# An LSTM feeding a sign-weight network on one core: the last quarter of the last block's outputs in two groups of four steps

## The chip, the cores and the metric

The kernel runs on one core of a Trainium2 chip. The metric is device time in microseconds. Of one execution there is also a profile, taken by the hardware profiler: every instruction of each engine with its start and length, the DMA packets, and the clock that TensorE was granted. A second run of the same kernel differs by a few tenths of a microsecond.

## What is computed

Inputs are 32 sequences of 64 steps of 256 numbers. An LSTM with 256 cells runs over the steps, and its hidden states go through three dense layers whose weights are signs; the result is added to the input.

```python
def lstm(x, h, Wx, Wh, b):              # x: (32, 64, 256)
    c = 0
    for t in range(64):
        i, f, o, g = split(x[:, t] @ Wx + b + h @ Wh, 4)
        c = sigmoid(f) * c + sigmoid(i) * tanh(g)
        h = sigmoid(o) * tanh(c)
        hs[:, t] = h
    return hs

def ffn(h, k0, k1, k2, s0, s1, s2):     # k: booleans, True = +1, False = -1
    a = relu(s0 * concat([h, -h]) @ sign(k0)) * 2     # 512 -> 1024
    a = relu(s1 * a @ sign(k1)) * 2                   # 1024 -> 1024
    return s2 * a @ sign(k2)                          # 1024 -> 256

out = x + ffn(lstm(x, cond, Wx, Wh, b), ...)
```

## The kernel before, in words

**Blocks.** The 64 steps are cut into four blocks of 16 steps (`SB`), that is 512 columns (`TB`; one column is one step of one sequence). The LSTM runs step by step; the network of block b runs on TensorE in the gaps of the LSTM of later blocks. The order of every engine's instructions is the order in which the program is written (`tc.manual_schedule()`), so a wait holds up whatever stands behind it on its engine.

**Precision.** The LSTM's products are in full float32. The network's are in a reduced float32 (`F32R`, 4 bytes, one pass of TensorE): each activation is split into a high and a low part (names ending in h and l), and each weight tile of 128 x 128 is multiplied by both. Every matmul in the profile is a pair of a weight load (LDWEIGHTS, engine column PEld) and a MATMUL (engine column PE). An instruction in full float32 appears as two such pairs.

**The last block.** The network of the last 16 steps (`last_block`) has no LSTM beside it any more; it is the end of the program. It works on two halves of eight steps (256 columns, `CB`). Its second layer is done by Strassen's method in quadrants (`product`, `take`, `take_sum`) and leaves the activations `a1[k, half]`, for eight tiles k and the two halves, as high and low tiles.

**The last layer of the last block**, where the change lies: the 256 outputs are two tiles m of 128, in the order that a 32 x 32 turn wants. `layer2(half, m, ...)` (L561) adds up, for one half and one m, eight tiles k times two parts: 16 matmuls of 256 columns. For the first half both m go into the two halves of one PSUM bank. For the second half m = 0 goes to a bank of `po`, and m = 1 to a bank of the pool `ps_f`. After that come, on VectorE, `turn_out` (L385, a transpose in 32 x 32 blocks from PSUM to SBUF) and `scale_out` (L388, times the product of the scales, plus the input x). The first half is turned twice, scaled once as 512 columns and stored while TensorE works on. In the second half each m is turned and scaled as soon as its 16 matmuls are done; when both are through, `store` (L380) sends the half out: four DMAs of 64 KB, one for each quarter of the 256 outputs, alternately from the queues of SyncE (SP) and ScalarE (ACT). Each is a set of pieces of 256 bytes.

```python
        for m in range(2):
            layer2(1, m, [*range(K2, FC0), *range(K2)], True, True)
            turn_out(os[1], po_half[1, m], m)
            scale_out(os[1][:, :, m, :], xq[b, 1][:, :, ts(m, 32)])
        store(b, 1, os[1].rearrange("p t m j -> p t (m j)"), [nc.sync, nc.scalar])
```

**After the last store** SyncE goes through all completion counters of the DMAs, one waiting instruction after another in a fixed order of counters, and then the engines meet twice (L764). Nothing of this is in the kernel's text. DMAs of the two hardware queues take their completion counters from eight in turn.

Of the kernel before, what the change touches and what calls it, by code (L numbers as in the profile page):

```python
# [32 lines left out]
F32 = mybir.dt.float32  # L33
# [8 lines left out]
def lstm_ffn(ctx: ExitStack, tc: tile.TileContext, x, cond, wx_d, wh_d, b_d, k0_d, k1_d, k2_d, s0_d, s1_d, s2_d, out):  # L42
    nc = tc.nc
    P = 128
    N, T, D = x.shape
# [3 lines left out]
    HQ = H // NQ  # L49
    F0 = k0_d.shape[1]  # L50
    F1 = k1_d.shape[1]
    FC0, FC1 = F0 // P, F1 // P
    SB = 16
    NB = T // SB
    TB = SB * N
# [22 lines left out]
    ps_f = ctx.enter_context(tc.tile_pool(name="ps_f", bufs=4, space=PSUM))  # L78
# [3 lines left out]
    def act(shape, dtype, name):  # L82
        return apool.tile(shape, dtype, tag="act", name=name)


    xq = {}
# [25 lines left out]
    first = warm[:, 4 : 4 + N]  # L112
# [47 lines left out]
    for i in range(2):  # L160
        t = act([P, 2, F0], U8, f"k0_{i}")
# [203 lines left out]
    def output(b, po):  # L365

        for half in range(2):
            o = act([P, SB // 2, 2, 32], F32, f"o{b}_{half}")
            for m in range(2):
                turn_out(o, po[m][:, ts(half, TB // 2)], m)  # L370
                yield
            o = o.rearrange("p t m j -> p t (m j)")
            scale_out(o, xq[b, half])
            store(b, half, o, [nc.sync])
            yield

    def store(b, half, o, engines):
        t0 = b * SB + half * (SB // 2)
        for q in range(NQ):
            engines[q % len(engines)].dma_start(  # L380
                out=out[:, t0 : t0 + SB // 2, ts(q, HQ)], in_=o[q * N : (q + 1) * N]
            )

    def turn_out(o, p, m):
        nc.vector.transpose(o[:, :, m, :], p.rearrange("p (t n) -> p t n", n=N))  # L385

    def scale_out(o, res):
        nc.vector.scalar_tensor_tensor(o, o, total, res, ALU.mult, ALU.add)  # L388


    K2, F2, CB = FC0 // 2, F1 // 2, TB // 2
# [25 lines left out]
    def last_block(b):  # L417

        hi, lo = hparts.pop(b)
        full, b11, b2, t, a1 = [], {}, {}, {}, {}  # L420
# [55 lines left out]
        for m in range(FC0):  # L476
            p = ps_f.tile([P, TB], F32, tag="pf", name=f"p0_{b}_{m}")
            for n, (k, a) in enumerate(((0, hi), (0, lo), (1, hi), (1, lo))):
                nc.tensor.matmul(p, w0[:, k, ts(m, P)], a[:, k, :], start=(n == 0), stop=(n == 3))  # L479
            f = act([P, 2, CB], F32, f"f_{m}")  # L480
            full.append(f)
            nc.scalar.activation(f.rearrange("p c n -> p (c n)"), p, AF.Relu)
            if m < K2:
# [3 lines left out]
                f = f[:, 0]  # L487
# [16 lines left out]
        q = [g.rearrange("p (i n) -> p i n", i=2) for g in gate_banks]  # L504
# [39 lines left out]
        for pair in range(2):  # L544
# [2 lines left out]

        po = [ps_o.tile([P, TB], F32, tag="po", name=f"po{b}_{m}") for m in range(2)]  # L550
        po_half = {
            (0, 0): po[0][:, :CB],
            (0, 1): po[0][:, CB:],
            (1, 0): po[1][:, :CB],
            (1, 1): ps_f.tile([P, TB], F32, tag="pf", name=f"po{b}_2")[:, :CB],
        }

        def layer2(half, m, ks, first, last):
            for k in ks:
                for n in range(2):  # L560
                    nc.tensor.matmul(  # L561
                        po_half[half, m],
                        w2[:, m, k],
                        a1[k, half][n],
                        start=first and k == ks[0] and n == 0 and (half, m) != (0, 1),
                        stop=last and k == ks[-1] and n == 1,
                        skip_group_check=True,
                    )

        os = [act([P, SB // 2, 2, 32], F32, f"o{b}_{half}") for half in range(2)]  # L570
        for ks in (range(K2), range(K2, FC0)):
            for m in range(2):
                layer2(0, m, ks, ks[0] == 0, ks[0] > 0)
        for m in range(2):
            turn_out(os[0], po_half[0, m], m)
        o = os[0].rearrange("p t m j -> p t (m j)")
        scale_out(o, xq[b, 0])
        store(b, 0, o, [nc.sync, nc.scalar])
        for m in range(2):
            layer2(1, m, [*range(K2, FC0), *range(K2)], True, True)  # L580
            turn_out(os[1], po_half[1, m], m)
            scale_out(os[1][:, :, m, :], xq[b, 1][:, :, ts(m, 32)])
        store(b, 1, os[1].rearrange("p t m j -> p t (m j)"), [nc.sync, nc.scalar])

    def ffn_block(b):
        hi, lo = hparts.pop(b)
# [98 lines left out]
    def ffn():  # L685
        for b in range(NB - 1):
            yield from ffn_block(b)
        yield from last_block(NB - 1)
# [13 lines left out]
    for t in range(T):  # L702
# [22 lines left out]
        else:  # L725
            if t >= FIRST_CHORE and chores:
                part = chores.popleft()()
# [40 lines left out]
```

## Time and profile before

| | |
|---|---|
| time, median of 3 runs | 312.36 us (312.21 to 312.55) |
| time of the profiled execution | 312.31 us |
| its span (first to last instruction) | 310.5 us |
| granted TensorE clock, mean | 0.998 |
| PE busy | 304.5 us, 98% of the span |
| PEld busy | 242.7 us, 78% |
| VectorE (DVE) busy | 178.1 us, 57% |
| ScalarE (ACT) busy | 142.0 us, 46% |
| matmuls of the last layer of the last block (L561) | 64, from 298.26 to 305.95 us |
| the program's last stores issued | 306.97 us and after |

The time of the profiled execution is longer than its span by 1.8 us, which lie before the first and after the last instruction. Matmuls overlap: the length of one is its passage through the array, and the rate is read from the distance between two starts. The ends of matmuls are modelled by the profiler. Starts are counted from the beginning of the span.

### The profile page before, as it was taken

Reading aid. Unit: us, or ns where it says so; the run is one execution under the profiler, and the core shown is the slowest. Engines: PE = TensorE matmul, PEld = TensorE weight load, DVE = VectorE, ACT = ScalarE, POOL = GpSimd, SP = SyncE. Lnnn points to the kernel's source line nnn. Section 1 sums busy time; section 2 is a strip of 40 time slices with the busy share of each in tenths; the row PEclk is TensorE's granted clock in tenths of the full one; section 3 lists DMA queues with packets and bytes.
Section 4 is the critical chain, followed back from the end, with each engine's and each line's share of the span. In section 5 each row is a group of like instructions: output and inputs, shape, how many; then the busy total and the mean of one; then the engine's idle time right before and its main releaser. Section 6 shows DMA issues by size and latency. Waiting matters only on the chain.

```text
span 310.5 us, 9798 instructions
## 1 busy us (share of the span) xinstructions
PE 304.5 (98%) x4138; PEld 242.7 (78%) x4138; DVE 178.1 (57%) x530; ACT 142.0 (46%) x512; POOL 6.6 (2%) x24
## 2 busy tenths in 40 slices
PE   8999999999999999999999999999999999999994
PEld 4888888788777777777777777777777777899993
DVE  2566767777673444355754445567554434698543
ACT  0225566774564543435633434355443333886220
POOL 5300000000000000000000000000000000000000
PEclk9999999999999999999999999999999999999999
DMA  6874001142000000000010000000310000131002
GB/s 192 206 196 99 5 19 38 36 95 65 3 2 0 2 2 0 3 2 0 2 38 22 14 3 0 2 2 13 92 34 2 3 0 2 31 79 27 2 0 69
DMA packets 30587, 10.89 MB, mean 35 GB/s; under 512 B 27720, under 2 KB 29768, under 8 KB 30544
## 3 DMA queue, kind: packets, MB, share of 16 engines
q1 hardware_dynamic: 27136, 8.66, 11.2%
q10 hardware_dynamic: 3168, 1.57, 2.0%
q8 instruction: 32, 0.52, 0.7%
q0 software_dynamic: 240, 0.04, 0.1%
q14 instruction: 11, 0.09, 0.1%
HBM read 8.16 MB, written 2.10 MB: 33 GB/s over the span
## 4 chain that ended last, share of the span: by engine, by line
PE 97%; DVE 1%; ACT 0%; issue 0%; ACTq 0%
PE p L617 30%; PE gates L305 20%; PE px L246 18%; PE p L591 8%; PE po L604 7%; PE gates L452 4%; PE po L561 2%; PE r L452 2%; PE x L452 2%; PE p L479 2%; PE p_idle L643 1%; PE gates L641 0%; DVE a_7l L362 0%; DVE o L388 0%; PE p_bias L658 0%
## 5 line engine op out<-in xcount | busy, mean ns | idle before, releaser
L305 PEld LDWEIGHTS gates<-wh,hist 128*32 128x32 f32 x2016 | 54.6, 109 | 22.3 <-issue 13.4
L305 PE MATMUL gates<-wh,hist 128*32 128x192 f32 x2016 | 68.1, 275 | 0.0
L246 PE MATMUL px<-wx,xT 128*32 128x256 f32 (+1 forms) x1168 | 60.5, 353 | 0.1
L322 ACT ACTIVATE sig<-gates 128x128 f32<-128x128 f32 x64 | 17.7, 277 | 80.6 <-PE gates L305 80.4
L246 PEld LDWEIGHTS px<-wx,xT 128*32 128x32 f32 x1168 | 42.4, 110 | 11.3 <-DVE c_first L652 0.7
L326 DVE TENSOR_TENSOR kept<-sig,c 128x64 f32<-128x64 f32 x63 | 14.2, 225 | 50.0 <-ACT sig L322 49.7
L332 ACT ACTIVATE th<-c 128x64 f32<-128x64 f32 x64 | 16.4, 257 | 31.4 <-DVE c L330 31.4
L334 DVE TENSOR_TENSOR h<-sig,th 128x64 f32<-128x64 f32 x64 | 14.4, 225 | 20.7 <-ACT th L332 20.7
L262 DVE TENSOR_TENSOR xg<-px,bias 128x512 f32<-128x512 f32 x32 | 21.2, 671 | 2.8 <-PE px L246 2.3
L316 ACT COPY gates<-xg 128x192 f32<-128x192 f32 x64 | 20.0, 313 | 1.3 <-DVE xg L262 1.3
L591 PE MATMUL p<-hhi,w 128*128 128x512 f32 x48 | 19.3, 402 | 0.0
L591 PE MATMUL p<-hlo,w 128*128 128x512 f32 x48 | 19.1, 398 | 0.0
L339 DVE STREAM_TRANSPOSE hist<-h 128x64 f32<-128x64 f32 x64 | 15.7, 245 | 2.4
L330 DVE TENSOR_TENSOR c<-kept,new 128x64 f32<-128x64 f32 x64 | 14.4, 224 | 2.2
L324 ACT ACTIVATE sig<-gates 128x64 f32<-128x64 f32 x64 | 14.9, 233 | 0.1
L323 ACT ACTIVATE cand<-gates 128x64 f32<-128x64 f32 x64 | 14.0, 218 | 0.0
L328 DVE TENSOR_TENSOR new<-sig,cand 128x64 f32<-128x64 f32 x64 | 13.9, 217 | 0.0
L317 ACT COPY gates<-xg 128x64 f32<-128x64 f32 x64 | 13.0, 203 | 0.0
L591 PEld LDWEIGHTS p<-hhi,w 128*128 128x128 f32 x48 | 9.0, 188 | 2.2
L591 PEld LDWEIGHTS p<-hlo,w 128*128 128x128 f32 x48 | 9.0, 188 | 2.0
L211 ACT ACTIVATE w<-bits,nsgn,sgn 128x1024 fp32r<-128x1024 uint8 x8 | 9.9, 1241 | 0.0
L617 PE MATMUL p<-a_7h,w 128*128 128x512 f32 x24 | 9.9, 413 | 0.0
(249 smaller groups left out, 602.8 us busy)
## 6 DMA issues: line engine op xcount, KB each, us to landing
x<-in_x_dram SPq DMA_DIRECT2D x60, 64.0 KB, 2.8
out_dram<-o SPq DMA_DIRECT2D x28, 64.0 KB, 1.8
bits<-in_L_ffn_k_dram SPq DMA_DIRECT2D x10, 128.0 KB, 3.2
wx<-in_L_cond_Wx_dram SPq DMA_DIRECT2D x2, 256.0 KB, 4.2
wx<-in_L_cond_Wx_dram ACTq DMA_DIRECT2D x4, 128.0 KB, 4.6
wh<-in_L_cond_Wh_dram ACTq DMA_DIRECT2D x2, 256.0 KB, 5.6
wh<-in_L_cond_Wh_dram SPq DMA_DIRECT2D x2, 256.0 KB, 6.2
k<-in_L_ffn_k_dram SPq DMA_DIRECT2D x2, 256.0 KB, 3.1
```

Source lines behind the costliest of these rows:

```text
L246: nc.tensor.matmul(p[q * N : (q + 1) * N, t % 2, slots], xT[i // 2, i % 2][:, s, k, :], wx_q[:, k, q, slots], start=start, stop=False, ski ...
L262: nc.vector.tensor_tensor(xg[t], p.rearrange("p t g j -> p t (g j)"), b, ALU.add)
L305: nc.tensor.matmul(g[q * N : (q + 1) * N], hT[:, k, :], wh_q[:, k, q, slots], start=False, stop=(k == 1), skip_group_check=True,)
L316: nc.scalar.copy(gates[0], x_t[:, :3])
L322: nc.scalar.activation(sig[:, 0:2, :], gates[0][:, 1:3], AF.Sigmoid)
L324: nc.scalar.activation(sig[:, 2, :], gates[1][:, 0], AF.Sigmoid)
L332: nc.scalar.activation(th, c, AF.Tanh)
L339: nc.vector.transpose(hT, h.rearrange("p (j b) -> p b j", b=2))
L452: nc.tensor.matmul(bank[pair][:, i], a(k)[:, ts(2 * pair + i, P)], b(k, n), start=first and i == 0 and k == 0 and n == 0, stop=last and k ...
L591: nc.tensor.matmul(p, w0[:, k, ts(m, P)], a[:, k, :], start=(n == 0), stop=(n == 3))
L604: nc.tensor.matmul(po[m], w2[:, m, k], a1[k][n], start=(k == 0 and n == 0), stop=(k == FC1 - 1 and n == 1))
L617: nc.tensor.matmul(p1[m], w1[:, k, ts(m, P)], a0[k][n], start=(k == 0 and n == 0), stop=(k == FC0 - 1 and n == 1),)
```

## The change

The m = 0 part of the second half stays as it was: 16 matmuls of 256 columns, one turn, one scaling. The m = 1 part ("the last half of the outputs of the last eight steps") is done in two groups of four steps, 128 columns each: 16 matmuls of 128 columns into a bank of its own, a turn of 128 columns, a scaling of 128 columns, and then a store of these four steps for all 256 outputs, four DMAs of 32 KB. Each group loads all its weights again. `store` takes the steps as a further argument, and `layer2` takes its target bank and its columns.

```diff
-    def store(b, half, o, engines):
+    def store(b, half, o, engines, part=slice(0, SB // 2)):
         t0 = b * SB + half * (SB // 2)
         for q in range(NQ):
             engines[q % len(engines)].dma_start(
-                out=out[:, t0 : t0 + SB // 2, ts(q, HQ)], in_=o[q * N : (q + 1) * N]
+                out=out[:, t0 + part.start : t0 + part.stop, ts(q, HQ)], in_=o[q * N : (q + 1) * N, part]
             )
...
         po = [ps_o.tile([P, TB], F32, tag="po", name=f"po{b}_{m}") for m in range(2)]
-        po_half = {
-            (0, 0): po[0][:, :CB],
-            (0, 1): po[0][:, CB:],
-            (1, 0): po[1][:, :CB],
-            (1, 1): ps_f.tile([P, TB], F32, tag="pf", name=f"po{b}_2")[:, :CB],
-        }
+        last_po = [ps_f.tile([P, TB], F32, tag="pf", name=f"po{b}_{2 + i}") for i in range(2)]

-        def layer2(half, m, ks, first, last):
+        def layer2(p, m, half, ks, first, last, cols=slice(0, CB)):
             for k in ks:
                 for n in range(2):
                     nc.tensor.matmul(
-                        po_half[half, m],
+                        p,
                         w2[:, m, k],
-                        a1[k, half][n],
-                        start=first and k == ks[0] and n == 0 and (half, m) != (0, 1),
+                        a1[k, half][n][:, cols],
+                        start=first and k == ks[0] and n == 0,
...
-        for m in range(2):
-            layer2(1, m, [*range(K2, FC0), *range(K2)], True, True)
-            turn_out(os[1], po_half[1, m], m)
-            scale_out(os[1][:, :, m, :], xq[b, 1][:, :, ts(m, 32)])
-        store(b, 1, os[1].rearrange("p t m j -> p t (m j)"), [nc.sync, nc.scalar])
+        o = os[1].rearrange("p t m j -> p t (m j)")
+        ks = [*range(K2, FC0), *range(K2)]
+        layer2(po[1][:, :CB], 0, 1, ks, True, True)
+        turn_out(os[1], po[1][:, :CB], 0)
+        scale_out(os[1][:, :, 0, :], xq[b, 1][:, :, :32])
+        for i in range(2):
+            steps, p = ts(i, SB // 4), last_po[i][:, : CB // 2]
+            layer2(p, 1, 1, ks, True, True, ts(i, CB // 2))
+            turn_out(os[1][:, steps], p, 1)
+            scale_out(os[1][:, steps, 1, :], xq[b, 1][:, steps, 32:])
+            store(b, 1, o, [nc.sync, nc.scalar], slice(i * SB // 4, (i + 1) * SB // 4))
```

The first half's calls of `layer2` and `turn_out` are written with the new arguments and do the same as before. After the change the lines of the last block move: `layer2`'s matmul is L557.

More of the change, by code (lines that the diff above doesn't have):

```diff
@@ L572, in last_block @@
             for m in range(2):
-                layer2(0, m, ks, ks[0] == 0, ks[0] > 0)
+                layer2(po[0][:, ts(m, CB)], m, 0, ks, ks[0] == 0 and m == 0, ks[0] > 0)
         for m in range(2):
-            turn_out(os[0], po_half[0, m], m)
+            turn_out(os[0], po[0][:, ts(m, CB)], m)
         o = os[0].rearrange("p t m j -> p t (m j)")
```

## The prediction

> **What bounds the kernel now.** I read the page first, its chain of work that ended last:
>
> ```profile
> PE 97%; DVE 1%; ACT 0%; issue 0%; ACTq 0%
> ```
>
> TensorE carries the chain to the end, and whatever it gains or loses in its last stage counts in full. So I asked for the chain from 298 us on:
>
> ```profile
> 298.26 7.69 PE po L561 x64
> 305.95 0.02 issue
> 305.98 0.46 DVE o L385
> 306.43 0.03 issue
> 306.46 0.48 DVE o L388
> ```
>
> The 64 matmuls of the last layer run without a gap for 7.69 us, 0.120 us each. Then the last turn and the last scaling follow one another, 0.46 and 0.48 us. The timeline of the end shows what hands over to what:
>
> ```profile
> 305.54 0.28 PE L561 MATMUL po<-c_1h,w 128*128 128x256 f32 x1
> ...
> 305.66 0.28 PE L561 MATMUL po<-c_1l,w 128*128 128x256 f32 x1
> 305.98 0.45 DVE L385 STREAM_TRANSPOSE o<-po 128x256 f32<-128x256 f32 x1 [0.95 <-PE po L561]
> 306.46 0.48 DVE L388 SCALAR_TENSOR_TENSOR o<-o,total,x 128x256 f32<-128x256 f32 x1
> 306.97 0.81 SPq L380 DMA_DIRECT2D out_dram<-o  x2
> 306.98 0.88 ACTq L380 DMA_DIRECT2D out_dram<-o  x2
> ```
>
> Starts of neighbouring matmuls are 0.12 us apart, the last begins at 305.66, and both queues issue two stores each, some 0.4 us per store. What follows is seen only in stretches of time (columns: length, busy engines, granted clock, DMA share, GB/s):
>
> ```profile
> 307.00:307.50 0.50, 0.00 (x0) 0.00 (x0) 0.00 (x0) 0.00 (x0) 0.00 (x0) 1.00 0.00 0
> 307.50:308.00 0.50, 0.00 (x0) 0.00 (x0) 0.00 (x0) 0.00 (x0) 0.00 (x0) 1.00 0.25 65
> 308.00:308.50 0.50, 0.00 (x0) 0.00 (x0) 0.00 (x0) 0.00 (x0) 0.00 (x0) 1.00 0.81 207
> 308.50:309.00 0.50, 0.00 (x0) 0.00 (x0) 0.00 (x0) 0.00 (x0) 0.00 (x0) 0.98 1.08 245
> 309.00:309.50 0.50, 0.00 (x0) 0.00 (x0) 0.00 (x0) 0.00 (x0) 0.00 (x0) 0.50 0.04 8
> ```
>
> Nothing moves until some 0.8 us after the issue; then the 256 KB take about 1.3 us at 200 to 250 GB/s, to 309.05 or so. Another 1.4 us go by until the span ends at 310.5. The end is thus a chain in series: matmuls, turn, scaling, issue, transfer, closing waits. The change makes the links after the matmuls shorter, and pays on TensorE.
>
> **TensorE: the term that decides.** Removed are 16 matmuls of 256 columns, added 32 of 128 columns with 16 weight loads more. The first of the 16 starts at 305.66 - 15 x 0.12 = 303.86. Before, the last one starts 15 x 0.12 = 1.80 us later; after, 31 x p, where p is the distance between starts at 128 columns. The trace has no reduced-float32 matmul of 128 columns, so p is bounded:
>
> - From below by streaming. The rows of 512 columns are 0.227 us apart (269.64, 269.87, 270.09 in L479), those of 256 columns 0.120. That is 0.107 per 256 columns and 0.013 fixed, which gives 0.067 at 128.
> - By the weight load. It is as long whatever the columns are. The groups by shape:
>
> ```profile
> L246 PEld LDWEIGHTS px<-wx,xT 128*32 128x32 f32 x1168 | 42.4, 110 | 11.3 <-DVE c_first L652 0.7 <-issue 0.4
> L591 PEld LDWEIGHTS p<-hlo,w 128*128 128x128 f32 x48 | 9.0, 188 | 2.0
> ```
>
> A load of 128 columns lasts 188 ns and one of 32 columns 110: 78 ns for 96 columns, 0.81 ns each, so 0.104 us of a full load are work that a second load can't share. Where TensorE starts after a wait, two loads stand directly behind one another:
>
> ```profile
> 81.03 0.19 PEld L591 LDWEIGHTS p<-hhi,w 128*128 128x128 f32 x1
> 81.03 0.50 PE L591 MATMUL p<-hhi,w 128*128 128x512 f32 x1
> 81.14 0.19 PEld L591 LDWEIGHTS p<-hlo,w 128*128 128x128 f32 x1
> ...
> 81.37 0.40 PE L591 MATMUL p<-hlo,w 128*128 128x512 f32 x1
> ```
>
> The second load starts 0.11 us after the first, though it waits for no data. At 256 columns the load (0.107) and the stream (0.107) are about equal, and the load hides; at 128 columns the stream is half as long and the load is not. I therefore expect p between 0.107 and 0.120 and take 0.112, near the row of two adjacent loads: 31 x 0.112 - 1.80 = **+1.67 us** (+1.52 to +1.92; by streaming alone +0.28). The last matmul's own passage is shorter by 128 of 256 columns: (0.389 - 0.283) / 2 = **-0.05**.
>
> The Trainium skill has a rule here that speaks against the change: "TensorE: Matmul & The Clock Gate", section "LDWEIGHTS (loading the stationary operand)", says that a load costs its columns over 1.2 GHz, whatever else is done, which is 0.107 us for 128; the loads 0.11 us apart agree. The same page, section "Back-to-back issue gap", gives about 0.081 us per matmul of 128 columns in a stream of loads and matmuls. By that figure the term would be an estimated +0.71 instead of +1.67, and my sum about +0.1 instead of +1.0; the two adjacent loads of this trace speak for the former.
>
> **VectorE.** The last turn is of 128 columns instead of 256. The rows: 245 ns at 64 columns (L339), 449 at 256, 1.06 ns per column, so -0.14. The last scaling: 752 ns at 512 columns, 484 at 256, 1.05 per column, so -0.13. Together **-0.27**. The first group's turn and scaling (about 0.32 + 0.35 us) cost nothing: TensorE meanwhile needs 16 x 0.112 = 1.8 us for the second group, in a bank of its own. m = 0 of this half is through at 305.03, before the first group's turn at about 305.8. Without that cover they would cost 0.67.
>
> **The transfer.** Four stores of 32 KB end the program instead of four of 64 KB. The first group's four are issued about 306.5, and at 0.4 us each two per queue are out by 307.4; the last four come about 308.3, so nothing queues behind them, and their packets (about 307.3 to 308.0) are over before the last ones' begin. Each queue's second store is issued 0.4 us after its first and starts moving 0.8 us later, thus not before 1.2 us; with 64 KB at 200 to 250 GB/s behind it, it ends some 1.5 us after the first issue instead of 2.1. The ends are 0 (if only fixed costs count) and -0.7 (if the time goes by bytes); I take **-0.55**, near the row by bytes, since the transfer is a solid block at full share.
>
> **The closing waits.** Eight completion counters are used in turn. With four stores more, the last store from ACT counts on another: read from the built instructions, on the one that SyncE waits for second and not sixth. All later waits are then behind the last landing. In the trace four such waits of L764 lie between 309.46 and 309.65, 0.06 us apart; four more are **+0.24** (0 to 0.3). The new waits of the last stores on the first half's stores are free: those were issued at 303.73 and moved by 306.0. The wait of the second group's bank is for a product of the second layer, long read.
>
> **Sum.** 1.67 - 0.05 - 0.27 - 0.55 + 0.24 = +1.04 us. On the profiled execution's 312.31 us this is 313.35; its median lies 0.05 higher, so I say 313.4 us, 0.33% slower, and the span 311.5. With the ends of the unknown costs this case reaches from +0.5 (1.52 - 0.05 - 0.27 - 0.7) to +1.8 (1.92 - 0.05 - 0.27 + 0.24), 312.8 to 314.2.
>
> **The rivals.**
>
> 1. *The load hides at 128 columns too.* Then p is 0.067 and the sum 0.28 - 0.05 - 0.27 - 0.55 + 0.24 = -0.35, or -0.74 with the best ends: 311.6 to 312.0, not slower. It decides from p = 0.078 downwards, where 31 p equals the 1.80 + 0.63 that the tail gives back. For it: the record of a load (192 ns) already overlaps the next at 0.120, so loads are pipelined in some part. Against it: two adjacent loads are never closer than 0.107 in this trace. Chance 0.12.
> 2. *Half-width matmuls lose the one-pass rate* and run like full float32. L246's 128 records of 128 columns take 4.03 us from 5.44 on, four at a time in separate column groups: 0.126 us per round, two records per product, 0.25 us. Then 31 x 0.25 - 1.80 = +5.95, the sum +5.3, 317.7 us (at 0.22, where the start of the kernel is not counted, +4.4). For it: no reduced-float32 matmul below 256 columns is in the trace, so nothing shows its rate. Against it: it is one instruction with the same type as its neighbours in the build, where full float32 is two. Chance 0.10.
> 3. *The tail doesn't shrink* because issue and landing, not bytes, set it: the main case without its 0.55, +1.6, 313.95 us. It lies in the main case's range, which has 0.78 in all.
>
> **How the numbers follow.** A measurement of this kernel tells apart about 0.2%, 0.62 us. The main case passes +0.62 in nearly nine parts of ten: 0.69 of its 0.78; with rival 2, slower is 0.79. The rest of the main case (0.09) and most of rival 1 (0.08) lie within 0.62 us: 0.17. The rest of rival 1, 0.04, is faster. The range goes from rival 1's middle, 312.0, to just above the main case's upper end, 314.3; outside are rival 2 (0.10), half of rival 1 (0.06) and a little for what I have not thought of.
>
> **What would show it.** In the timeline after: starts of the 128-column matmuls 0.107 to 0.120 us apart, with loads as far apart and PEld without gaps there; the last turn near 0.31 us and the last scaling near 0.35; two bursts of transfer, the second over about 1.5 us after its first issue; more of L764's waits behind the last landing. Starts 0.07 apart would make the prediction wrong to the fast side, two records per matmul or starts over 0.2 apart to the slow side; a second burst as long as before would move it to rival 3.

## The result

| | before | after |
|---|---|---|
| time, median of 6 runs each | 312.47 us (312.21 to 313.07) | 314.30 us (313.71 to 314.54) |
| ratio, 95% interval | | 1.0054 (1.0041 to 1.0067) |
| span of the profiled execution | 310.5 us | 312.5 us |

The change makes the kernel 0.5% slower. 313.4 us was predicted, with a range of 312.0 to 314.3.

### The profile page after: what moved, and what is told of

Read it like the earlier page. It is cut to its first block, busy times and chain, and to the rows that moved or that the text cites. A ratio compares the mean times of both kernels' runs of the same rounds, so it can differ in the third digit from the quotient of the medians.

```text
span 312.5 us, 9838 instructions
## 1 busy us (share of the span) xinstructions
PE 306.3 (98%) x4154; PEld 244.3 (78%) x4154; DVE 178.6 (57%) x532; ACT 142.1 (45%) x512; POOL 6.6 (2%) x24
## 4 chain that ended last, share of the span: by engine, by line
PE 95%; DMA 2%; DVE 1%; ACTq 0%; issue 0%; ACT 0%
PE p L619 30%; PE gates L305 20%; PE px L246 17%; PE p L593 8%; PE po L606 7%; PE gates L452 4%; PE po L557 3%; PE r L452 2%; PE x L452 2%; PE p L479 2%; DMA wx<-in_L_cond_Wx_dram 2%; ACTq L93 0%; DVE a_7l L362 0%; ACTq L127 0%; PE p_bias L660 0%
```

## The profile after

The page's chain still belongs to TensorE, now with a piece of DMA that was not in it before (it lies at the start of the program, as shown below):

```profile
PE 95%; DMA 2%; DVE 1%; ACTq 0%; issue 0%; ACT 0%
```

The end of the chain, from TensorE's last group on (start, length, what):

```profile
298.87 9.30 PE po L557 x80
308.17 0.02 issue
308.20 0.33 DVE o L385
308.52 0.03 issue
308.55 0.35 DVE o L388
```

80 matmuls in 9.30 us stand where 64 in 7.69 stood, which is +1.61. Turn and scaling have shrunk from 0.46 + 0.48 to 0.33 + 0.35. The timeline shows the rate, first where the shape changes and then at the end:

```profile
304.35 0.28 PE L557 MATMUL po<-c_1l,w 128*128 128x256 f32 x1
304.35 0.19 PEld L557 LDWEIGHTS po<-c_0h,w 128*128 128x128 f32 x1
304.47 0.22 PE L557 MATMUL po<-c_0h,w 128*128 128x128 f32 x1
304.47 0.19 PEld L557 LDWEIGHTS po<-c_0l,w 128*128 128x128 f32 x1
304.53 0.28 PE L557 MATMUL po<-c_0l,w 128*128 128x128 f32 x1
304.58 0.19 PEld L557 LDWEIGHTS po<-c_0h,w 128*128 128x128 f32 x1
304.64 0.27 PE L557 MATMUL po<-c_0h,w 128*128 128x128 f32 x1
...
306.41 0.32 DVE L385 STREAM_TRANSPOSE o<-po 128x128 f32<-128x128 f32 x1 [0.77 <-PE po L557]
306.76 0.35 DVE L388 SCALAR_TENSOR_TENSOR o<-o,total,x 128x128 f32<-128x128 f32 x1
...
307.77 0.28 PE L557 MATMUL po<-c_1h,w 128*128 128x128 f32 x1
307.82 0.19 PEld L557 LDWEIGHTS po<-c_1l,w 128*128 128x128 f32 x1
307.88 0.28 PE L557 MATMUL po<-c_1l,w 128*128 128x128 f32 x1
308.20 0.32 DVE L385 STREAM_TRANSPOSE o<-po 128x128 f32<-128x128 f32 x1 [1.08 <-PE po L557]
308.55 0.35 DVE L388 SCALAR_TENSOR_TENSOR o<-o,total,x 128x128 f32<-128x128 f32 x1
308.93 0.79 SPq L380 DMA_DIRECT2D out_dram<-o  x2
308.93 0.86 ACTq L380 DMA_DIRECT2D out_dram<-o  x2
```

At 256 columns a load starts together with the matmul before it, and both are 0.12 apart. From the second matmul of 128 columns on, the loads are 0.11 apart, each starts later than the matmul before it, and its own matmul follows 0.06 after the load's start instead of 0.12: the loads pace the engine. (The first gap between matmuls, 0.06, is this lead being used up once.) The first group's turn and scaling lie at 306.4 to 307.1 under the matmuls. What follows the last issue is again only to be seen by stretches (length, busy engines, granted clock, DMA share, GB/s):

```profile
309.50:310.00 0.50, 0.00 (x0) 0.00 (x0) 0.00 (x0) 0.00 (x0) 0.00 (x0) 0.59 0.35 86
310.00:310.50 0.50, 0.00 (x0) 0.00 (x0) 0.00 (x0) 0.00 (x0) 0.00 (x0) 0.50 0.58 138
310.50:311.00 0.50, 0.00 (x0) 0.00 (x0) 0.00 (x0) 0.00 (x0) 0.00 (x0) 0.50 0.18 39
```

128 KB move between 309.75 and 310.68, so for about 0.93 us; before, 256 KB took about 1.3. Half the bytes don't take half the time.

Now the links can be put side by side. A store lands when its completion counter is full; here that is the moment at which SyncE's wait for that counter ends. From the first matmul of the last quarter of the last layer (303.86 before, 304.47 after) to the end of the span:

| link, us | before | after |
|---|---|---|
| first to last matmul of the quarter | 1.80 | 3.41 |
| last matmul's start to last turn's start | 0.32 | 0.32 |
| last turn's start to last store's first issue | 1.00 | 0.73 |
| issue to last landing (to last packet) | 2.49 (2.12) | 2.26 (1.75) |
| last landing to the end | 1.07 | 1.32 |
| sum | 6.67 | 8.04 |

The stretch costs +1.37 us. The span grew by 2.0. The other 0.6 us is at the start, where the two kernels issue the same instructions. In the chain of waits of the kernel after:

```profile
2.19 5.80 DMA wx<-in_L_cond_Wx_dram
7.99 0.14 issue
8.13 1.95 PE px L246 x64
```

TensorE's second batch of 64 for the first product starts at 8.13, after a wait for a load of Wx; before, it starts at 7.51. From the bias matmul (9.26 before, 9.87 after) to the first matmul of the last quarter it is 294.6 us in both. The experiments show whether that shift belongs to the change.

## The experiments

Each kernel was profiled once and, but for one, timed in five rounds against the kernel before. The table has the same links for all (scaling in place of the turn where nothing is turned); "bias" is the start of the bias matmul, which stands for what the start of the kernel took.

| run | bias | first to last matmul | to last turn | turn to issue | issue to landing (last packet) | closing | sum | time against before, 95% |
|---|---|---|---|---|---|---|---|---|
| before | 9.26 | 1.80 | 0.32 | 1.00 | 2.49 (2.12) | 1.07 | 6.67 | |
| after | 9.87 | 3.41 | 0.32 | 0.73 | 2.26 (1.75) | 1.32 | 8.04 | 1.0054 (1.0041 to 1.0067) |
| after again | 10.18 | 3.41 | 0.32 | 0.73 | 2.22 (1.75) | 1.33 | 8.01 | 1.0044 (1.0032 to 1.0056) |
| matmuls alone | 9.16 | 3.41 | 0.31 | 1.00 | 2.50 (2.13) | 1.07 | 8.29 | 1.0063 (1.0051 to 1.0075) |
| rest alone | 9.54 | 1.80 | 0.94 | 1.00 | 2.28 (1.84) | 1.32 | 7.34 | 1.0018 (1.0009 to 1.0026) |
| light loads | 9.27 | 1.92 | 0.26 | 0.73 | 2.18 (1.77) | 1.32 | 6.42 | one run, 312.38 us |
| groups of 6 and 2 steps | 9.70 | 3.38 | 0.31 | 0.60 | 2.03 (1.59) | 1.32 | 7.65 | 1.0032 (1.0020 to 1.0044) |
| other counters | 9.91 | 3.41 | 0.32 | 0.73 | 2.20 (1.75) | 0.95 | 7.60 | 1.0045 (1.0033 to 1.0056) |
| a store for each m | 9.64 | 1.80 | 0.32 | 1.00 | 2.22 (1.80) | 1.32 | 6.66 | 1.0003 (0.9994 to 1.0011) |
| activations as weights | 9.04 | 1.78 | 0.31 | 0.51 | 2.84 (1.98) | 0.95 | 6.40 | 0.9990 (0.9981 to 0.9998) |
| the same, four instructions more | 9.79 | 1.78 | 0.32 | 0.51 | 2.10 (1.72) | 0.95 | 5.66 | 0.9966 (0.9953 to 0.9978) |
| the same, by sequence | 9.51 | 1.78 | 0.32 | 0.51 | 2.28 (1.92) | 0.95 | 5.85 | 0.9981 (0.9972 to 0.9990) |

**After again.** The kernel after, unchanged.

> The changed kernel once more, to see how much of its +2.0 us of span belongs to its end. In the first profile the end (from the first matmul of the last quarter to the end of the span) grew by 1.37 us (6.67 to 8.04), and the beginning (up to the first bias matmul) by 0.61 us (9.26 to 9.87), where TensorE waits for the weights Wx. Theory: the 0.61 us are chance of the loads at the start; the end is again 8.0 us, and the bias matmul starts anywhere between 9.2 and 10.0. Rival: the changed program starts later in every run; the bias matmul is at 9.8 to 9.9 again, and kernels with the same beginning as before (the third of this call) show 9.26.

The links come out the same within 0.04 us; the bias matmul comes at 10.18 instead of 9.87. In the twelve profiles it lies anywhere from 9.04 to 10.18 (wider than the 9.2 to 10.0 expected), among kernels that begin with the same instructions, early and late with the split matmuls (9.16, 10.18) and without (9.04, 9.79); from there to the last quarter it is 294.56 to 294.62 us in all but the last kernel of the table. So nothing ties the 0.6 us at the start to the change, and profiles are compared here by the sum of the links, not by their spans. What makes the start vary stays open; in the kernel after it is a load of Wx that TensorE waits for.

**Matmuls alone.** Two groups of matmuls, then turn, scaling and store as before.

```diff
-            layer2(p, 1, 1, ks, True, True, ts(i, CB // 2))
-            turn_out(os[1][:, steps], p, 1)
-            scale_out(os[1][:, steps, 1, :], xq[b, 1][:, steps, 32:])
-            store(b, 1, o, [nc.sync, nc.scalar], slice(i * SB // 4, (i + 1) * SB // 4))
+            layer2(p[:, ts(i, CB // 2)], 1, 1, ks, i == 0, True, ts(i, CB // 2))
+        turn_out(os[1], p, 1)
+        scale_out(os[1][:, :, 1, :], xq[b, 1][:, :, 32:])
+        store(b, 1, o, [nc.sync, nc.scalar])
```

> Only the matmuls are cut in two groups of 128 columns, into one bank; the turn, the scaling and the stores are whole as before. Theory: the spacing is 0.111 us, the last matmul starts 3.41 us after the first of the quarter instead of 1.80, and all that follows is as before: the end is 6.67 + 1.61 = 8.28 us, the whole +1.6 us against before, 0.25 more than the changed kernel's end. Rival (the second bank, or the wait on it, costs the spacing): below 0.1 us apart, end below 7.9 us.

The sum is 8.29, +1.62 on before, all of it in the first link. The whole time, 1.0063, is 1.97 us (1.60 to 2.35) of this call's 312.78 for before. So in the links this one part accounts for more than the whole loss, and the rest of the change gives back 0.25.

**Rest alone.** The last 16 matmuls whole, and after them the turns, scalings and stores by four steps.

```diff
+        layer2(p, 1, 1, ks, True, True)
         for i in range(2):
-            layer2(p, 1, 1, ks, True, True, ts(i, CB // 2))
-            turn_out(os[1][:, steps], p, 1)
+            turn_out(os[1][:, steps], p[:, ts(i, CB // 2)], 1)
```

> Only what follows the matmuls is cut in two groups of four steps; the 16 matmuls are whole as before. Theory: after the last matmul come turn, scaling, turn, scaling (2 x 0.70 instead of 1.00 us to the last issue), the transfer to its landing is shorter as in the changed kernel (2.26 instead of 2.49 us) and the closing waits are longer (1.32 instead of 1.07): the end is 6.67 + 0.40 - 0.23 + 0.25 = 7.1 us, +0.4 us. Rival (the tail's gain is real once the matmuls don't pay for it): 6.67 us or less.

Nothing covers the first group now. The chain of waits from 306 us on:

```profile
306.24 0.33 DVE o L385
306.57 0.03 issue
306.60 0.35 DVE o L388
306.95 0.24 DVE o L385
307.18 0.02 issue
307.21 0.35 DVE o L388
```

The second turn starts 0.62 later than the only turn before. And a cost came on top that I had left out: the scaling ends at 307.56, but SP's issue of the last store starts at 307.86, since SP is issuing the first group's stores until then; that is why "turn to issue" is 1.00 and not 0.70. The sum is +0.67. Smaller pieces at the end of a chain pay only if something covers the pieces before the last. TensorE's matmuls are that cover, and splitting them is what costs.

**Light loads.** After, but the weight tiles of the two groups have 64 columns instead of 128, except each group's first. It leaves 64 of the 128 outputs of this part unfinished.

```diff
+                    wide = P if not light or (k == ks[0] and n == 0) else P // 2
                     nc.tensor.matmul(
-                        p,
-                        w2[:, m, k],
+                        p[:wide],
+                        w2[:, m, k, :wide],
```

> The changed kernel, but of the 32 matmuls of 128 columns all except the first of each group load only 64 weight columns, so that 64 of the 128 outputs of the last quarter are left unfinished. Theory (the weight load sets the spacing): the load is half as long, starts come to 0.07 us apart (0.053 of streaming and 0.013 fixed), the 31 spacings take 2.1 to 2.3 us instead of 3.41. Rival (a matmul of 128 columns streams at half rate): starts stay 0.11 us apart, 3.4 us.

The timeline:

```profile
303.87 0.22 PE L558 MATMUL po<-c_0h,w 128*128 128x128 f32 x1
303.87 0.14 PEld L558 LDWEIGHTS po<-c_0l,w 128*64 128x64 f32 x1
303.93 0.22 PE L558 MATMUL po<-c_0l,w 128*64 128x128 f32 x1
303.93 0.14 PEld L558 LDWEIGHTS po<-c_0h,w 128*64 128x64 f32 x1
303.99 0.22 PE L558 MATMUL po<-c_0h,w 128*64 128x128 f32 x1
```

The same 128 columns stream, but with half the weight columns the matmuls are 0.060 us apart instead of 0.111, and load and matmul start together again. The one full load between the two groups stands out: the load behind it starts 0.109 later, the others 0.06. The edit halves a matmul's output rows together with its weight columns; for the load, and against the output, speak the two loads that the prediction shows at 81.03 and 81.14, 0.11 apart though the second waits for no result. So the weight load sets the 0.111, as the prediction said, and the sum is 6.42, 0.25 less than before: had the load been hidden, the change would have won by the links. The Trainium skill's page "TensorE: Matmul & The Clock Gate", section "LDWEIGHTS (loading the stationary operand)", has the rule that holds here (its 128 columns over 1.2 GHz are 0.107; measured 0.111). Its section "Back-to-back issue gap" gives 0.081 for 128 columns in a stream of loads and matmuls; for these 4-byte weights the trace has 0.111, and the measurement decides.

**Groups of 6 and 2 steps** instead of 4 and 4 (after with other bounds).

```diff
-        for i in range(2):
-            steps, p = ts(i, SB // 4), last_po[i][:, : CB // 2]
+        for i, (s0, s1) in enumerate(((0, 6), (6, 8))):
+            steps, p = slice(s0, s1), last_po[i][:, : (s1 - s0) * N]
```

> The changed kernel with groups of six and two steps (192 and 64 columns) instead of four and four. Theory (the load sets the spacing, whatever the columns below 256): 0.111 us in both groups, the last matmul 3.41 us after the first; turn and scaling of 64 columns are 0.07 us shorter each, the last stores of 16 KB land some 0.1 to 0.2 us earlier: end 7.7 to 7.8 us. Rival (the spacing goes with the columns, at half rate): 0.17 us at 192 and 0.07 at 64, the last matmul 3.7 to 3.8 us after the first.

The timeline in the second group, at 64 columns:

```profile
306.89 0.28 PE L557 MATMUL po<-c_0h,w 128*128 128x64 f32 x1
307.00 0.28 PE L557 MATMUL po<-c_0l,w 128*128 128x64 f32 x1
307.11 0.28 PE L557 MATMUL po<-c_0h,w 128*128 128x64 f32 x1
```

Behind each group's first gap, starts are 0.109 to 0.116 apart at 192 columns and 0.111 to 0.112 at 64. Rival 2 (a lower rate below 256 columns) is out: what a matmul streams, from 64 to 192 columns, doesn't matter here. Once the matmuls are paid for twice, the last group may as well be small: its shorter tail makes the sum 7.65 instead of 8.04, still 0.98 above before.

**Other counters.** After, with six of the eight loads of x for the last block cut in two, so that the last stores take the counters that SyncE waits for last.

```diff
-            load_x(b, half, [nc.sync])
+            ...
+            for q in range(NQ):
+                for part in (slice(0, 4), slice(4, 8)) if q < 3 else (slice(0, 8),):
+                    nc.sync.dma_start(out=xq[b, half][q * N : (q + 1) * N, part], in_=...)
```

> The changed kernel with six more loads of x some 30 us before the end (six of the last block's eight loads are cut in two), which only moves the last stores to other completion counters: ScalarE's last store counts on the one that SyncE waits for last but one, not second. Theory (a later counter in the closing round saves 0.061 us each): from the last landing to the end of the span 1.32 - 6 x 0.061 = 0.95 us, the end of the kernel 7.65 us instead of 8.03. Rival (the closing stretch is a fixed 1.3 us, or is set by the landing itself): unchanged, 8.0 us.

The closing falls from 1.32 to 0.95, six waits of 0.061 us that now lie ahead of the last landing. SP's waits from 308 us on, after first, then this kernel (who waited for what, us in total, times, longest):

```profile
SPq L766 <- DMA out_dram<-o: 1.4, 1, 1.4
```

```profile
SPq L773 <- DMA out_dram<-o: 0.9, 2, 0.5
```

One long wait, with seven counters behind it, has become two, the second of them with one counter behind it. In the sum of the links it is -0.41 on the run "after again". The whole time doesn't show it (1.0045 against 1.0044, each within 0.0012, that is 0.37 us): the mechanism is shown by the profile, its worth in the whole time is not.

**A store for each m.** On the kernel before: each m is stored as soon as it is scaled, in pieces of 128 bytes, so that the last stores carry half the bytes, without any change to the matmuls.

```diff
             scale_out(os[1][:, :, m, :], xq[b, 1][:, :, ts(m, 32)])
-        store(b, 1, os[1].rearrange("p t m j -> p t (m j)"), [nc.sync, nc.scalar])
+            store_m(b, 1, os[1], m, [nc.sync, nc.scalar])
```

> The kernel before, whole matmuls, but each m of the second half is stored by itself as soon as it is scaled: four DMAs of 32 KB in pieces of 128 bytes for m = 0, beside the matmuls of m = 1, and four at the end. The last stores have half the bytes and as many pieces. If the transfer goes by bytes, it lands 2.26 us after the first issue as in the changed kernel (2.49 before), and with 0.25 us more of closing waits the end is 6.67 - 0.23 + 0.25 = 6.7 us, no change. If it goes by pieces, 2.49 us and 6.9 us, 0.25 us slower than before.

The last packet comes 1.80 us after the issue: as after (1.75, as many bytes in pieces of 256), not as before (2.12, as many pieces but twice the bytes). So the number of pieces is not what counts. The gain of 0.27 in landing is paid out again: four more stores move the last one to another counter, closing +0.25. Sum and time are those of before.

**Activations as weights.** On the kernel before: the last half is computed the other way round. The 128 columns of four steps are the stationary operand and the 256 outputs move. A group of four steps then costs 16 matmuls of 256 columns, both groups 32, as many as before; the result has a row for each step and sequence and needs no turn.

```diff
+                        a1[k, 1][n][:, ts(i, CB // 2)],
+                        w2[:, :, k].rearrange("p m (q j) -> p q m j", q=NQ),
...
+            nc.vector.scalar_tensor_tensor(o[:, i], p, total, x_rows[:, i], ALU.mult, ALU.add)
+            for s in range(SB // 4):
+                (nc.sync, nc.scalar)[s % 2].dma_start(out=rows[:, s], in_=o[ts(s, N), i])
```

> The kernel before with the last half's products turned round: 128 columns of activations (four steps) are loaded as weights, and the 256 outputs of one weight tile stream past them. Two groups of four steps of 16 matmuls with 256 columns each, as many matmuls as before in this half; results come out with one row per step and sequence, so the turn is left out, x is read and the result stored by rows of 1 KB, four DMAs of 32 KB per group, and the last two counters of the closing round are used. Theory (a matmul that streams 256 columns hides its load): starts 0.120 us apart, 1.80 us from the group's first to its last; then 0.32 to the scaling, 0.49 of scaling, about 2.0 from issue to landing (four stores of 32 KB in 32 pieces), 0.95 of closing: end 5.6 us from the last quarter's first matmul instead of 6.67, 1.1 us faster than before. Rival (a load that reads activations or a stream over the two halves of the weight tile costs more): starts over 0.13 us apart, which takes the gain from 0.155 on.

The matmuls are 0.119 apart and the store is issued 0.50 us sooner than before (2.61 against 3.11 after the first matmul of the quarter), but it lands 2.84 after its issue, some 0.6 later than the stores of 128 KB above, and the sum is 6.40 instead of the 5.6 expected. The profile of its DMAs between 307.3 and 308.3 us (queue, kind: packets, MB, share) has a guest in the last store's transfer:

```profile
q10 hardware_dynamic: 83, 0.05, 19.9%
q1 hardware_dynamic: 50, 0.03, 10.7%
q14 instruction: 1, 0.01, 3.3%
```

One packet of 8 KB of queue 14, an instruction fetch, occupies one DMA engine from 307.41 to 307.93. Every kernel has one in its last microseconds; in the others above it comes at 305.6 to 306.6, before the last store moves. In the kernels before and after and in four others (light loads, matmuls alone, rest alone, a store for each m) it comes 1.1 us after VectorE has begun the m = 0 scaling of the second half (not the first half's, as my next expectation has it), which made VectorE's code the suspect.

**The same, four instructions more.** VectorE makes each low part of the second half in two instructions instead of one, well ahead of the end; nothing else is changed.

```diff
-            nc.vector.scalar_tensor_tensor(l, p, 0.0, h, ALU.max, ALU.subtract)
+            for i in range(2) if half == 1 else [slice(0, 2)]:
+                nc.vector.scalar_tensor_tensor(l[:, i], p[:, i], 0.0, h[:, i], ALU.max, ALU.subtract)
```

> The run with activations as weights with one difference: VectorE makes each low part of the second half in two instructions instead of one (four more VectorE instructions, under TensorE's matmuls), nothing else. Theory A: the DMA that fetches instructions, which came at 307.41 us in the middle of the last store (in the other kernels at 305.6 to 306.6, about 1.0 us after VectorE had made the last scaling of the first half), fetches VectorE's code and delayed the last landing: with four instructions more ahead it starts near 305 to 306, before the last store moves, and the last store lands 2.1 to 2.3 us after its issue instead of 2.84, so that the end is 5.7 to 5.9 us after the first matmul of the last quarter instead of 6.40, ratio about 0.997. Theory B: the fetch is for another engine: it stays at 307.4 and the end at 6.4. Theory C: the fetch moves, but the landing stays 2.8 us after the issue, since the stores write pieces of 1 KB that are 64 KB apart: end 6.4, ratio 0.999.

The DMAs of this kernel, from 304.5 to 305.1 us and from 307 to 309.1:

```profile
q14 instruction: 1, 0.01, 3.8%
```

```profile
q10 hardware_dynamic: 115, 0.07, 12.7%
q1 hardware_dynamic: 101, 0.07, 11.3%
```

The fetch now comes at 304.60, and the last store has its time to itself: it lands 2.10 after the issue, the last packet at 1.72. The sum is 5.66, 0.74 less than without the four instructions, and the time is 0.9966 of before. This is the fastest kernel of the study, about 1.1 us below before. Theory A holds, though the fetch came earlier than the 305 to 306 expected. All twelve traces agree with it: counted in VectorE's instructions, waits included, this fetch always follows the start of the 574th, by 1.1 to 1.3 us in eleven kernels and by 1.7 in the one without the four instructions, where the 574th is the last scaling. The Trainium skill's page "Runtime: NRT & Kernel Launch", section "Instruction fetch mechanics", calls the cost of running over a block of code mostly hidden; here it went with 0.74 us, paid not by the engine that fetched, but by a store in the same DMA engines. Only 0.26 of it is the later last packet; after that the landing took 0.86 instead of 0.38. The counters say where: each store is counted in sixteen steps, as many as the core has DMA engines. Without the four instructions 62 of the last four stores' 64 steps are in by 2.14 us after the first issue, and one step of each queue's second store follows at 2.64 and 2.82; with them all 64 are in by 2.09. That is what one held-up engine of sixteen would leave, but the trace does not say which engine carried the fetch, and why these two steps come over 0.6 us after the last recorded packet is not settled.

The chain of waits shows what TensorE and VectorE now do at the end; the turn is gone:

```profile
302.62 3.82 PE po L589 x32
306.44 0.02 issue
306.47 0.48 DVE o_rows L597
```

**The same, by sequence.** Also with four instructions more, and the columns of the second half written in the order sequence, step, so that a group is 16 sequences of 8 steps and goes out in two DMAs of 64 KB, one from each queue, instead of four of 32 KB.

```diff
+            if half == 1:
+                p = p.rearrange("p i (t n) -> p i t n", n=N)
+                ho, lo = (a.rearrange("p i (n t) -> p i t n", n=N) for a in (h, l))
...
+            rows = out[ts(i, N // 2), t0 : t0 + SB // 2]
+            for s, engine in enumerate([nc.sync, nc.scalar]):
+                engine.dma_start(out=rows[:, :, ts(s, P)], in_=o[:, i, ts(s, P)])
```

> As the run with activations as weights (built on the kernel before): the last half is computed with the activations as the stationary operand and the weights as 256 moving columns, so that the result lies in PSUM with the columns (step, sequence) as partitions and the 256 outputs as elements, and needs no turn. New: the columns of the second half are written in the order sequence, step (VectorE then makes each low part in two instructions, four more in all), so that a group is 16 sequences of 8 steps, and its 128 KB go out in two DMAs of 64 KB, one from each queue, instead of four of 32 KB from strips 64 KB apart. From the first matmul of the last quarter to the end (6.67 us before, 8.04 after the change, 6.40 with activations as weights): if the tail of the changed kernel is held up by the second issue of each queue (0.36 to 0.42 us), the last packet comes 1.35 to 1.5 us after the first issue (1.75 after the change with the same bytes, 1.98 with activations as weights) and the landing at 1.85; then 1.80 + 0.31 + 0.51 + 1.85 + 0.95 = 5.4 us, 1.2 us less than before, ratio about 0.996. If the bytes set it: last packet at 1.75, landing 2.2, end 5.8, ratio 0.997. If the late landing of the run with activations as weights comes from having each sequence in pieces of its own far apart or from the instruction fetch falling into the transfer whatever the layout, the landing stays near 2.8 and the end near 6.4, ratio 0.999.

I had thought that the second issue of each queue holds the tail up. Leaving it out did not shorten the tail: with one issue per queue the last packet comes at 1.92, later than with two (1.72). Issuing one of these DMAs takes 0.58 us, and its first packet comes 1.25 us after the issue instead of 0.82. What was saved on the second issue went into the first. It isn't the size alone: the kernel before has DMAs of 64 KB too, from 32 partitions in pieces of 256 bytes, and its first ones are issued in 0.32 and 0.38 us and move 0.83 us after the issue; these here come from 128 partitions in pieces of 512 bytes. Which of the two it is stays open. The strided writing costs too, earlier on: ScalarE's

```profile
L471 ACT ACTIVATE c_1h<-v 128x512 fp32r<-128x512 f32 x1 | 1.2, 1245 | 2.0 <-DVE v L478 2.0
```

takes 1245 ns where the same instruction into plain order takes 632, and the way to the last quarter is 0.33 us longer (294.92). Faster than before; by the links and this way it is slower than the kernel without the new order (5.85 and 0.33 against 5.66), while in the whole time the two intervals overlap (0.9972 to 0.9990, 0.9953 to 0.9978).

## Why the prediction was right, and where it was off

The sum of the prediction was +1.04 us, its links measured +1.37; the whole time moved by 1.7 (1.3 to 2.1) in the first comparison, 1.83 between the medians, and by 1.4 (1.0 to 1.75) in the second. The 314.30 us lie on the upper end of the stated range and above the main case's own end of 314.2 (314.26, had its closing waits been taken at their 0.3 and not at 0.24). The direction and the terms were foreseen; that this one comparison stayed inside the range was partly luck.

- **What bounds the kernel:** right. TensorE carries the chain, and what it pays in the last stage counts in full: matmuls alone +1.62 in the links.
- **TensorE, +1.67 by starts 0.112 apart:** right in size and cause. They are 0.109 to 0.115 apart behind the first gap, and the link is +1.61. The cause, the weight load, is shown by light loads and by groups of 6 and 2.
- **The last matmul's own passage, -0.05:** wrong, 0.00. I read it from records of matmuls whose loads had long been done. Here they wait for their loads inside their records, 0.27 to 0.28 us instead of the 0.22 of the first, and from the start of the last to the turn it is 0.32 as before; in light loads, where the load is hidden, it is 0.26.
- **VectorE, -0.27:** right. The turn takes 317 ns instead of 449, the scaling 352 instead of 485, and the first group's hide under the matmuls. Rest alone shows what the cover is worth.
- **The transfer, -0.55:** the mis-sized term: -0.23 measured. Two things were wrong in "ends some 1.5 us after the first issue instead of 2.1". I let each queue's second store start moving 0.8 us after its issue; from ACT, the later queue, it begins about 1.0 after it: the four DMAs begin to move 0.82, 0.98, 1.31 and 1.44 after the first issue, one behind another. And the rate of 200 to 250 GB/s was a mean over a burst of four overlapping DMAs, which I then took for the price of a byte: one DMA moves for 0.39 to 0.51 us with 64 KB and still for 0.29 to 0.34 with 32 KB, and the pause between the two of a queue grew from 0.08 and 0.12 to 0.17 and 0.19. The last packet comes 1.59, 1.75 and 2.12 us after the issue for 64, 128 and 256 KB: 0.16 to 0.19 us per 64 KB on a floor of some 1.4. So 128 KB less are worth 0.37, and the lag from the last packet to the landing, 0.37 before and 0.51 after (0.47 after again), takes part of that back. By sequence, with one issue per queue in another form, did not get below this floor.
- **The closing waits, +0.24:** right, +0.25, and other counters takes them away again.
- **The rivals:** the load does not hide (light loads is what it would have been), and half-width matmuls keep their rate. Two readings behind the first were not exact: streaming allows 0.060 at 128 columns (light loads), not 0.067, and "never closer than 0.107" holds for the 4-byte loads of 128 columns, while two bf16 loads at 1.24 us start 0.015 apart. Neither enters the main sum. The third, a tail that does not shrink, was half true: the transfer gave 0.23 of its 0.55.

Put together, -0.05 and -0.55 that came as 0.00 and -0.23 are +0.37, less 0.06 on TensorE: 0.31 of the 0.33 by which the links exceed the forecast. The first comparison's interval holds the links' +1.37, so nothing more has to be explained there; what its middle shows above that is of the size of the starts' scatter.

## What to carry to other kernels

Cutting the last stage into smaller pieces shortens what follows TensorE, but with a stationary tile of 128 columns there is a width (here between 192 columns, which are paced by the load, and 256) below which a matmul costs its weight load whatever it streams; look first whether the operands can be exchanged, so that the same pieces come with as many loads as before. Price a shorter transfer by its marginal bytes, from two sizes in the trace, not by the mean rate of a burst. Compare small changes at the end by the links from a common point, because in these profiles the start of the program scatters by 1.1 us, nearly as much as the change moves.

## What was not expected of the hardware

- With an instruction fetch of 8 KB in the last store's transfer the program's end took 0.74 us longer, and four VectorE instructions more or less, far ahead, decided whether the fetch fell there.
- The price of issuing a store goes with its form: 64 KB from 128 partitions in pieces of 512 bytes took 0.58 us to issue and moved 1.25 us after it, 64 KB from 32 partitions in pieces of 256 bytes 0.32 us and 0.83.
- ScalarE writing with a stride of eight elements takes 1173 to 1245 ns for what takes 632 in plain order.
